# A four-layer graph network on one core: turns without loops, gather buffers of five groups, scatters in batches of five groups

## The chip, the cores and the metric

The kernel runs on one core of a Trainium2 chip. The metric is the device time of one execution in microseconds (us); less is better. The core has five engines that each work through their own queue in order: TensorE (PE, with its weight loads listed as PEld), VectorE (DVE), ScalarE (ACT), GpSimd (POOL) and SyncE (SP), which here only starts DMAs. Indirect DMAs (gathers and scatters by a list of row numbers) are issued by POOL, all others by SP.

## What is computed

A graph has N = 12500 nodes with 32 features each and E = 400000 edges (`src`, `dst`), sorted by `dst`. Four message-passing layers follow each other, each with a residual and a layer norm:

```python
edge_index = jnp.stack([src, dst])
x = _layernorm(x + _L0_gnn_ref(x, edge_index, edge_weight1, edge_attr_3, edge_attr_5, L0_gnn_W), axis=-1)
x = _layernorm(x + _L1_gnn_ref(x, edge_attr_2, L1_gnn_weight, edge_index), axis=-1)
x = _layernorm(x + _L2_gnn_ref(x, edge_index, edge_attr_2, L2_gnn_g, L2_gnn_mu, L2_gnn_sigma, L2_gnn_root, L2_gnn_bias), axis=-1)
x = _layernorm(x + _L3_gnn_ref(x, edge_weight, edge_attr_3, edge_index, L3_gnn_w1, L3_gnn_b1, L3_gnn_w2, L3_gnn_b2), axis=-1)
```

Layers 0, 2 and 3 read a row of `x` per edge at `src` and add a message at `dst`: layer 0 multiplies the row with spherical harmonics of the edge and mixes by small matrices, layer 2 weighs it by three Gaussians of the edge's two attributes (and takes a mean, a root matrix and a bias), layer 3 multiplies it with a matrix that a small network makes from the edge's distance. Layer 1 goes the other way:

```python
# _L1_gnn_ref
xj = x[edge_index[1]]                       # rows at dst
msg = basis[:, 0:1] * (xj @ w2[0])
for k in range(1, k1 * k2):                 # 16 products of tent functions
    msg = msg + basis[:, k:k + 1] * (xj @ w2[k])
out = jax.ops.segment_sum(msg, edge_index[0], num_segments=n_nodes)   # added at src
```

## The kernel before

An edge tile is P = 128 edges; T = 5 tiles are a group, G = 25 groups a turn, and NG = 25 turns are all edges. Since the edges are sorted by target, the targets of a group fit in a window of W = 64 nodes; a wider group would be done again under `If(wide)` (L469), which this data never enters.

**Layers 0, 2 and 3** share `edge_pass` (L330). `begin(i)` copies the turn's source indices, relative targets and window starts from tables of the whole graph (`src_all`, `rel_all`, `base_i`) into small tiles by DVE (L343, L345, L349; two buffers each) and calls the layer's `prepare`. For every group, `gathered` (L352) has POOL gather 5 x 128 rows of `x` into an `xg` tile (L356; six buffers). In layers 0 and 2, ACT copies `xg` to PSUM as `xp` (L414). `one_hot` has DVE make the group's 128 x 64 target one-hots (`hot`, L372; four buffers); layer 0 also stores them to HBM, `hot_d`, from where layer 3 loads them. DVE makes the per-edge product (layer 0: `prod`, L625 and L631; layer 2: L855), PE multiplies it with the one-hots (L386), and DVE adds the result to the running sums in SBUF, `acc`, at a column that it reads from the base tile (L406).

Layer 0's `prepare0` also computes the basis of layer 1, in `basis_rows` (L575): `d` on DVE (L579), two activations on ACT (L585, L586), `basis` on DVE (L589), transposes on PE (L604), copies on ACT (`bs`, L608 to L611), and stores to `basis_d` by SP. Layer 3 has a radial network on PE (`pr`, L971, biases set by ACT at L966), a product and a sum on DVE (L986, L998), and runs one group ahead.

The turns are in a hardware loop over NG // U, with U = 5 turns written out inside:

```python
def turns(j):
    begun = begin(j * U)
    for k in range(U):
        now = begun
        for s in range(G):
            if s == G // 2 and k + 1 < U:
                begun = begin(j * U + k + 1)
            yield j * U + k, s, now

with tc.For_i(0, NG // U, 1) as j:
    run(turns(j))
```

**Layer 1** first multiplies every node's row with all 16 matrices (`y_d`). Then `turn1` (L697) goes through a turn. For each group SP loads basis rows (`bas`), relative targets (`rel`), five slices of `y_d` (`yw`, at offsets read from `pairs`) and source rows (`row`). ACT copies `rel` to PSUM (`rel_p`, L723; one buffer), DVE makes basis-weighted one-hots from it (`bm`, L726, two per group), PE multiplies them with `yw` (`pe`, L744, ten matmuls), ACT copies the messages (`msg`, L752). Edges of one tile with an equal source are summed by PE (`pm`, L774, with `same` of L758), and all but one of such edges are sent to a spare row: DVE works out the destinations `to` (L762 to L770). ACT copies the sums (`add`, L776; four buffers), and POOL adds the five tiles to five copies of the result in HBM, `sums[t]`, by five indirect DMAs (L778). Its loop is like the one above (L786). A later pass, `node_pass`, adds the copies up.

A scheduler sets the order of the instructions on each engine when the program is built, by estimated times; waits between engines follow from which tile is read and written. Inside a loop's body it may move instructions of one turn into another, but not past the loop's ends.

Of the kernel before, what the change touches and what calls it, by code (L numbers as in the profile page):

```python
# [10 lines left out]
F32 = mybir.dt.float32  # L11
I32 = mybir.dt.int32
AF = mybir.ActivationFunctionType
ALU = mybir.AluOpType
# [6 lines left out]
P = 128  # L21
F = 32
T = 5
G = 25
W = 64
U = 5
V = 16
EPS_LN = 1e-5

# [10 lines left out]
def kernel(  # L40
# [25 lines left out]
    nc = tc.nc  # L66
    N = x_in.shape[0]
    NG = src_t.shape[0]
    GT = G * T
# [27 lines left out]
        out=before,  # L97
        in_=before,
        compare_op=ALU.is_gt,
        fill=0.0,  # L100
        base=0,
# [8 lines left out]
    base_i = const.tile([1, NS], I32, name="base_i")  # L110
    src_all = const.tile([P, NG, GT], I32, name="src_all")
    rel_all = const.tile([P, NG, GT], F32, name="rel_all")
# [52 lines left out]
    nid = const.tile([P, 2], F32, name="nid")  # L165
# [89 lines left out]
    with (  # L255
# [10 lines left out]
        for c, n in ((0, 124), (1, 124)):  # L266
# [10 lines left out]
            for idx, (_, _, lo) in enumerate(COMBOS):  # L277
                for k in range(3 if lo else 1):
                    to = wc0[:n, c, 8 + k : F : 3] if lo else wc0[:n, c, 0:8]
# [39 lines left out]
    src_c = nodes.tile([P, GT], I32, name="src_c")  # L319
    rel_c = nodes.tile([P, G, T], F32, name="rel_c")  # L320
    base_c = nodes.tile([1, G], I32, name="base_c")
# [8 lines left out]
    def edge_pass(layer, pools, acc, prepare, product, chunks, xg_psum=False):  # L330
# [5 lines left out]
        io, work, ps_agg, ps_x = pools  # L336
# [2 lines left out]
        nc.vector.memset(acc, 0.0)  # L339

        def begin(i):
            src = io.tile([P, GT], I32, name="src")
            nc.vector.tensor_copy(src, src_all[:, ds(i, 1), :].rearrange("p a g -> p (a g)"))  # L343
            rel = io.tile([P, G, T], F32, name="rel")
            nc.vector.tensor_copy(  # L345
                rel.rearrange("p g t -> p (g t)"), rel_all[:, ds(i, 1), :].rearrange("p a g -> p (a g)")
            )
            base = io.tile([1, G], I32, name="base")
            nc.vector.tensor_copy(base, base_i[:, ds(i * G, G)])  # L349
            return src, rel, base, prepare(i)  # L350

        def gathered(s, begun):  # L352
            xg = work.tile([P, T, F], F32, name="xg", bufs=6)
            src = begun[0]
            for t in range(T):
                nc.gpsimd.indirect_dma_start(  # L356
                    out=xg[:, t, :],
                    out_offset=None,
                    in_=x_dram[layer],
                    in_offset=bass.IndirectOffsetOnAxis(  # L360
                        ap=src[:, s * T + t : s * T + t + 1], axis=0
                    ),
                )
            return xg

        def one_hot(i, s, begun, first):
            hot = work.tile([P, T, W], F32, name="hot", bufs=4)
            kept = hot_d[ds(i * G + s, 1)].rearrange("a p t w -> (a p) t w")
            if first and layer == 3:
                nc.sync.dma_start(hot, kept)  # L370
                return hot
            nc.vector.tensor_tensor(  # L372
                hot,
                iota_w[:, None, :].to_broadcast([P, T, W]),
                begun[1][:, s, :, None].to_broadcast([P, T, W]),
                ALU.is_equal,
            )
            if first and layer == 0:
                nc.sync.dma_start(kept, hot)
            return hot  # L380
# [14 lines left out]
        def add_up(s, begun, agg, adds):  # L395

            with tc.issue_after(adds[-1].ins) if adds else nullcontext():
                at = nc.values_load(
                    begun[2][0:1, s : s + 1],
                    engines=[DVE],  # L400
                    min_val=0,
                    max_val=N,
                    skip_runtime_bounds_check_because="a target's index or N, by the min below",
                )
            cols = acc[:, :, ds(at, W)]
            adds.append(nc.vector.tensor_tensor(cols, cols, agg, ALU.add))  # L406

        def run(groups, first=True):
            adds = []
            for i, s, begun in groups:  # L410
                xg = gathered(s, begun)
                if xg_psum:
                    xp = ps_x.tile([P, T, F], F32, name="xp")
                    nc.scalar.copy(xp, xg)  # L414
                    xg = xp
                hot = one_hot(i, s, begun, first)
                prod = product(begun[3], i, s, xg)
                add_up(s, begun, aggregate(prod, hot), adds)
# [28 lines left out]
        if isinstance(product, tuple):  # L447
            run = run_ahead

        def turns(j):  # L450
            begun = begin(j * U)
            for k in range(U):
                now = begun
                for s in range(G):
                    if s == G // 2 and k + 1 < U:
                        begun = begin(j * U + k + 1)
                    yield j * U + k, s, now

        with tc.For_i(0, NG // U, 1) as j:
            run(turns(j))  # L460


        wide = nc.values_load(
# [4 lines left out]
        )  # L468
        with tc.If(wide > 0):  # L469
            with tc.For_i(0, NG, 1) as i:  # L470
                src, rel, base, _ = begin(i)
                nc.vector.tensor_copy(rel_c, rel)
                nc.vector.tensor_copy(src_c, src)
                nc.vector.tensor_copy(base_c, base)
                n_win = nc.values_load(
                    wins_i[0:1, ds(i, 1)],
                    min_val=1,
                    max_val=(N - 1) // W + 1,
                    skip_runtime_bounds_check_because="a span of targets, which are below N",
                )  # L480
                with tc.For_i(0, n_win, 1):
                    nc.vector.tensor_scalar(rel_c, rel_c, float(W), None, op0=ALU.subtract)
                    nc.vector.tensor_scalar(
                        base_c, base_c, float(W), float(N), op0=ALU.add, op1=ALU.min
                    )
                    prep = prepare(i)
                    run([(i, s, (src_c, rel_c, base_c, prep)) for s in range(G)], first=False)
# [79 lines left out]
    with ExitStack() as sums_es:  # L567
      acc0 = sums_of(sums_es, 0, 124, 2)
      with ExitStack() as es:
        pools = layer_pools(es, 0)  # L570
        io, work = pools[:2]
# [50 lines left out]
        def product0(sh, i, s, xg):  # L622
# [14 lines left out]
            return prod  # L637

        edge_pass(0, pools, acc0, prepare0, product0, [(0, 124), (124, 248)], xg_psum=True)
      node_pass(0, acc0, [wc0[:124, 0, :], wc0[:124, 1, :]])  # L640

# [6 lines left out]
    sums = [dram.tile([N + P, F], F32, name=f"sums{t}") for t in range(T)]  # L648
    with ExitStack() as es:
        io = es.enter_context(tc.tile_pool(name="yio", bufs=2))  # L650
# [34 lines left out]
    with ExitStack() as es:  # L685
        io = es.enter_context(tc.tile_pool(name="io1", bufs=2))
        one = es.enter_context(tc.tile_pool(name="one1", bufs=1))
        work = es.enter_context(tc.tile_pool(name="work1", bufs=2))
# [5 lines left out]
        def load_pairs(i, to):  # L694
            nc.sync.dma_start(to, pair_d[ds(i * GT, GT)].rearrange("(a t) -> a t", a=1))

        def turn1(i, pairs, ids):  # L697
            src_f = ps_s.tile([P, G, T], F32, name="src_f")
            nc.vector.tensor_copy(
                src_f.rearrange("p g t -> p (g t)"), src_all[:, ds(i, 1), :].rearrange("p a g -> p (a g)")  # L700
# [3 lines left out]
                spare, past[:, None, :].to_broadcast([P, G, T]), src_f, ALU.subtract  # L704
            )
            for s in range(G):
                e0 = i * (G * SE) + s * SE

                def spread(of):
# [10 lines left out]
                rel = work.tile([P, T, P], F32, name="rel", bufs=3)  # L720
# [45 lines left out]
                nc.vector.tensor_reduce(later, dup, AX.X, ALU.max)  # L766
                to_f = work.tile([P, T], F32, name="to_f")
                nc.vector.tensor_tensor(to_f, later, spare[:, s, :], ALU.mult)
                to = work.tile([P, T], I32, name="to", bufs=4)
                nc.vector.tensor_tensor(to, to_f, src_f[:, s, :], ALU.add)  # L770

                pm = ps_m.tile([P, T, F], F32, name="pm")
                for t in range(T):
                    nc.tensor.matmul(pm[:, t, :], same[:, t, :], msg[:, t, :], start=True, stop=True)  # L774
                add = work.tile([P, T, F], F32, name="add", bufs=4)
                nc.scalar.copy(add, pm)  # L776
                for t in range(T):
                    nc.gpsimd.indirect_dma_start(  # L778
                        out=sums[t],
                        out_offset=bass.IndirectOffsetOnAxis(ap=to[:, t : t + 1], axis=0),  # L780
                        in_=add[:, t, :],
                        in_offset=None,
                        compute_op=ALU.add,
                    )

        with tc.For_i(0, NG // U, 1) as j:  # L786
            for k in range(U):
                i = j * U + k
                pairs = io.tile([1, GT], I32, name="pairs")
                load_pairs(i, pairs)  # L790
                turn1(i, pairs, nid)


        over = nc.values_load(
# [26 lines left out]
    with ExitStack() as sums_es:  # L821
      acc2 = sums_of(sums_es, 2, 97, 1)
      with ExitStack() as es:
        pools = layer_pools(es, 2)
        io, work = pools[:2]
        one = es.enter_context(tc.tile_pool(name="one2", bufs=1))
# [42 lines left out]
    with ExitStack() as sums_es:  # L869
      acc3 = sums_of(sums_es, 3, 80, 1)  # L870
      with ExitStack() as es:
        pools = layer_pools(es, 3, agg_bufs=1, x_bufs=0)
        io, work = pools[:2]
# [253 lines left out]
```

## Time and profile before

| | us |
|---|---|
| median of 3 runs | 19965.96 |
| lowest and highest | 19964.43, 19989.18 |
| profiled execution | 19970.15 |
| its span, first to last instruction | 19968.4 |

Busy time in the profiled span:

| engine | busy us | share | instructions |
|---|---|---|---|
| PE | 12304.1 | 62% | 51816 |
| DVE | 9989.9 | 50% | 17389 |
| ACT | 3741.9 | 19% | 8543 |
| POOL | 13975.9 | 70% | 12511 |

The span falls into stages, which can be told apart by the lines that run: layer 0 from 117.69 to 4299.60 us, layer 1 from 4678.56 to 10782.50 (with the layer norm and the making of `y_d` before it), layer 2 from 10892.36 to 14860.70, layer 3 from 15055.40 to 19882.70. Shares of the whole span hide which engine is full in which stage, so the profile is read by stage. In a timeline, each line has the start, the duration, the engine, the line of the program, what it writes and reads, and in brackets how long the engine had been idle and what ended that; `issue` means that the profile shows no event that it waited for.

### The profile page before, as it was taken

Reading aid. Unit: us, or ns where it says so; the run is one execution under the profiler, and the core shown is the slowest. Engines: PE = TensorE matmul, PEld = TensorE weight load, DVE = VectorE, ACT = ScalarE, POOL = GpSimd, SP = SyncE. Lnnn points to the kernel's source line nnn. Section 1 sums busy time; section 2 is a strip of 40 time slices with the busy share of each in tenths; the row PEclk is TensorE's granted clock in tenths of the full one; section 3 lists DMA queues with packets and bytes.
Section 4 is the critical chain, followed back from the end, with each engine's and each line's share of the span. In section 5 each row is a group of like instructions: output and inputs, shape, how many; then the busy total and the mean of one; then the engine's idle time right before and its main releaser. Section 6 shows DMA issues by size and latency. Waiting matters only on the chain. (4 is left out here: it accounts for less than half of the span.)

```text
span 19968.4 us, 200494 instructions
## 1 busy us (share of the span) xinstructions
PE 12304.1 (62%) x51816; PEld 9777.9 (49%) x51817; DVE 9989.9 (50%) x17389; ACT 3741.9 (19%) x8543; POOL 13975.9 (70%) x12511
## 2 busy tenths in 40 slices
PE   4666667677767767677674222222246767777776
PEld 4666666665666666666664222222233333333333
DVE  3333333323444444444444222222229999999998
ACT  0000000001111111111110000000004545445454
POOL 5777767745878878788786777777756665666664
PEclk9975555555555555555555555555556777777777
DMA  2121211115766767677674000000002222222222
GB/s 57 46 50 45 49 47 48 48 55 134 129 123 129 129 122 129 123 129 129 122 129 91 14 15 14 15 15 14 14 11 56 56 58 53 60 55 58 55 58 48
DMA packets 1944708, 1361.88 MB, mean 68 GB/s; under 512 B 1123399, under 2 KB 1691663, under 8 KB 1938192
## 3 DMA queue, kind: packets, MB, share of 16 engines
q1 hardware_dynamic: 1193443, 1142.31, 21.9%
q0 software_dynamic: 750000, 205.60, 11.9%
q8 instruction: 441, 7.23, 0.2%
q14 instruction: 824, 6.75, 0.1%
HBM read 1127.27 MB, written 219.34 MB: 67 GB/s over the span
## 5 line engine op out<-in xcount | busy, mean ns | idle before, releaser
L356 POOL DMA_INDIRECT xg<-x,src x6250 | 6112.7, 978 | 2938.6 <-issue 1480.4
L386 PE MATMUL agg<-hot,prod 128*124 128x64 f32 (+1 forms) x18750 | 3868.7, 400 | 4161.7 <-DVE prod L855 2822.5
L778 POOL DMA_INDIRECT sums<-add,to x3125 | 4863.3, 1556 | 1645.1 <-issue 1084.5
L386 PEld LDWEIGHTS agg<-hot,prod 128*124 128x124 f32 (+1 forms) x18750 | 3686.5, 309 | 4351.0 <-issue 4285.4
L356 POOL DMA_INDIRECT xg<-in_x_in,src x3125 | 2998.6, 960 | 1232.2 <-issue 792.3
L744 PE MATMUL pe<-yw,bm 128*128 128x32 f32 x12500 | 2926.3, 403 | 1460.1 <-DVE bm L726 1403.1
L744 PEld LDWEIGHTS pe<-yw,bm 128*128 128x128 f32 x12500 | 2758.2, 328 | 1629.7 <-DVE bm L726 1495.6
L971 PE MATMUL pr<-wr,h 64*128 64x512 f32 x6250 | 2800.5, 926 | 821.0 <-ACT pr L966 735.2
L726 DVE SCALAR_TENSOR_TENSOR bm<-rel_p,nid,bas 128x640 f32<-128x640 f32 x1250 | 1090.6, 881 | 3253.4 <-ACT rel_p L723 3253.4
L406 DVE TENSOR_TENSOR acc<-acc,agg 124x128 f32 (+2 forms) x1875 | 448.7, 239 | 3215.8 <-PE agg L386 3211.0
L971 PEld LDWEIGHTS pr<-wr,h 64*128 64x128 f32 x6250 | 968.5, 275 | 2090.4 <-ACT pr L966 1353.4
L986 DVE TENSOR_TENSOR big<-pr,fa 128x1024 f32<-128x1024 f32 x1875 | 1838.3, 1032 | 24.1 <-ACT fa L958 20.0
L966 ACT COPY pr<-b2r 128x1024 f32<-128x1024 f32 x1875 | 1594.1, 872 | 1076.4 <-DVE big L986 1035.1
L998 DVE TENSOR_REDUCE msg<-big 128x160 f32<-128x2560 f32 x625 | 1754.2, 2807 | 0.2
L414 ACT COPY xp<-xg 128x160 f32<-128x160 f32 x1250 | 370.3, 296 | 7242.7 <-DMA xg<-x,src 3654.2
L774 PE MATMUL pm<-msg,same 128*128 128x32 f32 x6250 | 1464.7, 403 | 272.0 <-ACT msg L752 272.0
L774 PEld LDWEIGHTS pm<-msg,same 128*128 128x128 f32 x6250 | 1380.5, 329 | 356.2 <-ACT msg L752 356.2
L855 DVE TENSOR_TENSOR prod<-gauss,xp 128x480 f32<-128x480 f32 x625 | 408.5, 654 | 1890.9 <-ACT xp L414 1842.4
L386 PEld LDWEIGHTS agg<-hot,msg 128*80 128x80 f32 x6250 | 596.8, 177 | 1220.6 <-DVE acc L406 1187.0
L386 PE MATMUL agg<-hot,msg 128*80 128x64 f32 x6250 | 692.3, 268 | 570.0 <-DVE acc L406 538.5
L752 ACT COPY msg<-pe 128x160 f32<-128x160 f32 x625 | 182.8, 293 | 3734.3 <-PE pe L744 3734.3
L372 DVE TENSOR_TENSOR hot<-consts,rel 128x320 f32<-128x320 f32 x1250 | 601.4, 484 | 176.6 <-DMA hot_d<-hot 176.6
(166 smaller groups left out, 7408.1 us busy)
## 6 DMA issues: line engine op xcount, KB each, us to landing
bas<-basis_d SPq DMA_DIRECT2D x625, 320.0 KB
rel<-rel_d SPq DMA_DIRECT2D x625, 320.0 KB
row<-in_src_n SPq DMA_DIRECT2D x625, 320.0 KB
hot_d<-hot SPq DMA_DIRECT2D x625, 160.0 KB
yw<-y_d SPq DMA_DIRECT2D x3125, 32.0 KB
xg<-x,src POOLq DMA_INDIRECT x6250
hot<-hot_d SPq DMA_DIRECT2D x625, 160.0 KB
dist<-in_ew_n SPq DMA_DIRECT2D x625, 96.0 KB
```

The lines of the kernel that those rows point to most:

```text
L356: nc.gpsimd.indirect_dma_start(out=xg[:, t, :], out_offset=None, in_=x_dram[layer], in_offset=bass.IndirectOffsetOnAxis(ap=src[:, s * T + ...
L372: nc.vector.tensor_tensor(hot, iota_w[:, None, :].to_broadcast([P, T, W]), begun[1][:, s, :, None].to_broadcast([P, T, W]), ALU.is_equal,)
L386: nc.tensor.matmul(agg[:, c, :], prod[:, t, a:b], hot[:, t, :], start=(t == 0), stop=(t == T - 1),)
L406: adds.append(nc.vector.tensor_tensor(cols, cols, agg, ALU.add))
L726: nc.vector.scalar_tensor_tensor(bm[:, h], rel_p, ids[:, h : h + 1], bas, op0=ALU.is_equal, op1=ALU.mult)
L744: nc.tensor.matmul(pe[:, t, :], bm[:, h, t, :], yw[:, t, h * F : (h + 1) * F], start=(h == 0), stop=(h == 1),)
L774: nc.tensor.matmul(pm[:, t, :], same[:, t, :], msg[:, t, :], start=True, stop=True)
L778: nc.gpsimd.indirect_dma_start(out=sums[t], out_offset=bass.IndirectOffsetOnAxis(ap=to[:, t : t + 1], axis=0), in_=add[:, t, :], in_offset ...
L966: nc.scalar.copy(pr[:, : b - a, :], b2r.rearrange("p o u j -> p (o u j)")[:, None, :].to_broadcast([P, b - a, 512]),)
L971: nc.tensor.matmul(pr[:, k, :], h[64 * k : 64 * k + 64, a // 2, :], wr[64 * k : 64 * k + 64].rearrange("h o u j -> h (o u j)"), start=Fals ...
L986: nc.vector.tensor_tensor(big[:, a * 4 : b * 4], pr[:, : b - a, :].rearrange("p t (o u j) -> p (t o) u j", u=8, j=16), fa[:, a * 4 : b * 4 ...
L998: nc.vector.tensor_reduce(msg[:, :, 0:32], big.rearrange("p (t o) u j -> p t (o u) j", o=4), AX.X, ALU.add,)
```

## The change

All 25 turns are written out in all four layers, and no loop is left on the path that the data takes. `begin` makes no copies: gathers, one-hots and window starts are read from the whole-graph tables. The `xg` buffers hold five groups each and there are three of them, so 15 groups in place of six. Layer 0 has eight `hot` buffers. In layer 1 the scatters of five groups are issued together, 25 in a row, each made to depend on the last `add` and the last `to` of the five; `adds` and `tos` hold five groups in three buffers each. Only the first five groups of all are still added one by one.

```diff
-U = 5
+B = 5
...
         def begin(i):
-            src = io.tile([P, GT], I32, name="src")
-            nc.vector.tensor_copy(src, src_all[:, ds(i, 1), :].rearrange("p a g -> p (a g)"))
-            rel = io.tile([P, G, T], F32, name="rel")
-            nc.vector.tensor_copy(
-                rel.rearrange("p g t -> p (g t)"), rel_all[:, ds(i, 1), :].rearrange("p a g -> p (a g)")
-            )
-            base = io.tile([1, G], I32, name="base")
-            nc.vector.tensor_copy(base, base_i[:, ds(i * G, G)])
-            return src, rel, base, prepare(i)
+            rel = rel_all[:, i, :].rearrange("p (g t) -> p g t", t=T)
+            return src_all[:, i, :], rel, base_i[:, i * G : (i + 1) * G], prepare(i)
+
+        batch = [None]

         def gathered(s, begun):
-            xg = work.tile([P, T, F], F32, name="xg", bufs=6)
+            if s % B == 0:
+                batch[0] = work.tile([P, B, T, F], F32, name="xg", bufs=3)
+            xg = batch[0][:, s % B]
...
-            hot = work.tile([P, T, W], F32, name="hot", bufs=4)
+            hot = work.tile([P, T, W], F32, name="hot", bufs=8 if layer == 0 else 4)
...
-        with tc.For_i(0, NG // U, 1) as j:
-            run(turns(j))
+        run(turns())
...
+        def after(ins, other):
+            tc.add_manual_dep(
+                ins.ins,
+                other.ins.name,
+                mybir.DependencyInfo(mybir.DependencyClass.Sync, mybir.DependencyReason.DATA),
+                reason="one wait for what several would be waited for",
+            )
...
+                if s % B == 0:
+                    adds = work.tile([P, B, T, F], F32, name="adds", bufs=3)
+                    tos = work.tile([P, B, T], I32, name="tos", bufs=3)
+                    ready = []
+                add, to = adds[:, s % B], tos[:, s % B]
...
-                to = work.tile([P, T], I32, name="to", bufs=4)
-                nc.vector.tensor_tensor(to, to_f, src_f[:, s, :], ALU.add)
+                to_i = nc.vector.tensor_tensor(to, to_f, src_f[:, s, :], ALU.add)
...
-                add = work.tile([P, T, F], F32, name="add", bufs=4)
-                nc.scalar.copy(add, pm)
-                for t in range(T):
-                    nc.gpsimd.indirect_dma_start(
...
+                ready.append((nc.scalar.copy(add, pm), to_i))
+                if len(ready) < (1 if first and s < B else B):
+                    continue
+                for k in range(s % B + 1 - len(ready), s % B + 1):
+                    for t in range(T):
+                        into = nc.gpsimd.indirect_dma_start(
+                            out=sums[t],
+                            out_offset=bass.IndirectOffsetOnAxis(ap=tos[:, k, t : t + 1], axis=0),
+                            in_=adds[:, k, t, :],
+                            in_offset=None,
+                            compute_op=ALU.add,
+                        )
+                        for last in ready[-1]:
+                            after(into, last)
+                ready = []
...
-        with tc.For_i(0, NG // U, 1) as j:
-            for k in range(U):
-                i = j * U + k
-                pairs = io.tile([1, GT], I32, name="pairs")
-                load_pairs(i, pairs)
-                turn1(i, pairs, nid)
+        for i in range(NG):
+            pairs = io.tile([1, GT], I32, name="pairs")
+            load_pairs(i, pairs)
+            turn1(i, pairs, nid, first=i == 0)
```

`turns` now runs over all NG turns, and the body under `If(wide)` makes its own copies of the indices.

## The prediction

> **What bounds the kernel now.** I read first the busy time by stage, cutting the span where the work changes. Columns: stretch, its length, busy time (with count) of PE, PEld, DVE, ACT and POOL, granted PE clock, DMA share, GB/s. The four long rows are layers 0, 1, 2, 3; what lies between and around them sums to 887 us.
>
> ```profile
> 117.69:4299.60 4181.91, 2792.70 (x12900) 2684.58 (x12900) 1416.26 (x2622) 296.74 (x805) 2998.57 (x3125) 0.64 0.19 47
> ...
> 4678.56:10782.50 6103.94, 4383.40 (x18718) 4131.58 (x18718) 2685.12 (x4414) 742.33 (x1871) 4863.30 (x3125) 0.50 0.70 126
> ...
> 10892.36:14860.70 3968.34, 1163.95 (x6250) 1066.84 (x6250) 891.09 (x2042) 203.60 (x655) 2973.58 (x3125) 0.50 0.09 14
> ...
> 15055.40:19882.70 4827.30, 3477.72 (x12490) 1562.94 (x12486) 4737.31 (x7986) 2414.71 (x5007) 3121.03 (x3106) 0.72 0.25 56
> ```
>
> Layers 0 and 2 look alike: POOL has 3125 gathers and nothing else is near full. Layer 3 is DVE's (4737 of 4827 us). In layer 1 no engine is full. Then I read POOL's timeline (start, duration, what, idle before it and what ended that).
>
> ```profile
> 953.92 0.97 POOL L356 DMA_INDIRECT xg<-in_x_in,src  x1 [27.81 <-DVE base L349]
> 955.20 0.94 POOL L356 DMA_INDIRECT xg<-in_x_in,src  x1 [0.30 <-issue]
> ...
> 1793.33 0.97 POOL L356 DMA_INDIRECT xg<-in_x_in,src  x1 [27.76 <-DVE base L349]
> ...
> 12480.24 0.94 POOL L356 DMA_INDIRECT xg<-x,src  x1 [10.16 <-DVE base L349]
> 13275.24 0.94 POOL L356 DMA_INDIRECT xg<-x,src  x1 [10.15 <-DVE base L349]
> ...
> 16973.85 0.94 POOL L356 DMA_INDIRECT xg<-x,src  x1 [52.46 <-DVE base L349]
> 17941.94 0.95 POOL L356 DMA_INDIRECT xg<-x,src  x1 [51.87 <-DVE base L349]
> ```
>
> A gather is 0.945 + 0.303 us = 1.25, so a loop iteration of 625 takes POOL 780 us at best. The iterations are 839.4 (layer 0), 795.0 (2) and 968.1 (3). At every loop boundary POOL stands still until DVE has copied the new turn's indices (`base` L349 is the last of those copies).
>
> **The change, part by part.**
>
> Layer 0. Above 3125 x 1.25 = 3906 us the stage has 249 us of POOL idle and slow gathers before its end tail. From the timeline: four boundaries of 27.7 to 27.8 behind a first iteration, 109.8 us with what follows each; 20 stalls of up to 6.7 us, one in nearly every turn, 96.1 us; gathers of 2 to 3 us in place of 0.945, 49.6 us. The stall is this:
>
> ```profile
> 2119.70 0.24 DVE L343 COPY src<-src_all 128x125 int32 x1 [26.14 <-DMA xg<-in_x_in,src]
> 2130.64 0.94 POOL L356 DMA_INDIRECT xg<-in_x_in,src  x1 [6.27 <-ACT xp L414]
> ```
>
> The copy of the next turn's indices may not overwrite `src` before the gathers that read it have landed. DVE is in order, so `prod` behind the copy is late, `xp` of ACT waits for `prod`, and the six `xg` tiles fill. The change removes the copies (the gathers read `src_all`) and puts 15 groups in `xg`. The consumer needs 5.56 us a group where it isn't waiting, against POOL's 6.25, so it catches up 17 us in a turn, and 15 groups cover 94 us. I take off the boundaries (no loop: -110) and the stalls (-96); the slow gathers stay. One more wait could hold one-hots: their stores queue on SP behind the 12 to 16 stores of `basis_d`, up to 25 us in the waits (DVE hot <- DMA hot_d<-hot). Eight tiles of `hot` cover 8 x 6.25 = 50 us of that.
>
> Start of layer 0. The first gather is at 117.69, because `base` is copied after all of the preamble on DVE; in the changed program's order it waits only for the load of `src_all` (in by about 25 us, an estimate from the first DVE work on a load, at 25.41). 75 gathers can run before the first buffer must be free: 25 + 94 = 119. What DVE does meanwhile may slow them, and here a rule must be weighed. By the trace, some gathers are slow beside DVE operations that read two operands in SBUF: at 968.93 one takes 2.94 us beside `basis` (2.23 us). The preamble has some 15 us of such operations, all now beside gathers: `rel_all` 3.40, `rel_p` 3.49, and `d` (1.2) three times and `basis` (2.2) twice. So the 76th gather comes at about 135. The Trainium skill (SBUF — State Buffer, "Who interferes with whom") says otherwise: a tensor_tensor with both inputs in SBUF takes only the read interface of the shared ports, and descriptor generation, which needs the write interface, is inferred to go on. By that rule it is 125, set by ACT's fifth `xp` copy, which follows the memset of `acc` (93.2 to 114.2 before). I take the row: 135; should the 21 us memset hold gathers too, which nothing here shows, 155. Before, the 76th gather was at 117.69 + 94 + 5 = 217. So -82 (-62 to -92). Layer 0: -110 - 96 - 82 = -288.
>
> Layer 1. POOL's waits in the page read `issue`, which looks like overhead that batching would save. The timeline says otherwise:
>
> ```profile
> 8012.62 0.15 DVE L770 TENSOR_TENSOR to<-to_f,src_f 128x5 int32<-128x5 f32 x1
> 8013.50 1.55 POOL L778 DMA_INDIRECT sums<-add,to  x1 [0.60 <-issue]
> ...
> 8020.67 0.70 ACT L723 COPY rel_p<-rel 128x640 f32<-128x640 f32 x1
> ...
> 8022.20 0.15 DVE L770 TENSOR_TENSOR to<-to_f,src_f 128x5 int32<-128x5 f32 x1
> ...
> 8023.09 1.55 POOL L778 DMA_INDIRECT sums<-add,to  x1 [0.59 <-issue]
> ```
>
> A group's first scatter comes 0.73 us after its `to` has ended, in nearly every group. Had POOL been the bound, that lag would grow. The pitch is 9.59 us; five scatters are 5 x (1.556 + 0.303) = 9.30. What gives 9.59 is a loop through ACT's queue: `add` of group s (0.29), `rel_p` of s+1 (0.70), wait for `bm` and `pe` (5.97), `msg` (0.29), wait for `pm` (2.43): 9.7 with the overlaps. The waits carry it:
>
> ```profile
> ACT msg L752 <- PE pe L744: 3728.4, 624, 6.1
> ```
>
> Inside a turn the changed program keeps ACT, DVE, PE and SP in this same order, so the pitch stays and one wait for 25 scatters in place of five waits is worth nothing: 25 x 1.859 + 0.29 = 46.8 us per batch against 5 x 9.59 = 47.95. It nearly reaches it: scatters of over 1.6 us busy would make POOL the bound. POOL has nothing else queued, nobody but ACT and DVE wants the tiles back, and three buffers leave them two batches of room. Two changes remain: the four boundaries (25.9 to 27.4 idle in POOL) go, -106; and the last batch starts only when its fifth group is ready, so 25 scatters (46.5) follow it instead of five (9.3), +37. Layer 1: -69. Bounds: if half of each boundary comes back because SP's loads can't run ahead, -16; if the last groups' scatters cost nothing extra, -106.
>
> Layer 2: four boundaries of 8.6 to 10.2, -38. The 24 us of slow gathers stay.
>
> Layer 3: an iteration is 968.1 where five undisturbed turns of 190.2 make 951; the POOL gap of 52 us is covered by gathers that ran ahead, and DVE loses about 18 in refilling. Four times, -72; the three copies per turn (0.23, 0.22, 0.17, overlapping to 0.4) are on DVE, the bound, 25 times: -10. Layer 3: -82.
>
> Between the stages the loads of layer 1's first turn and the preparations of layers 2 and 3 no longer stand behind a loop's entry: -5, -8 and -8, guesses from how long the first group of each took. The tail of 85.7 stays.
>
> Sum: -288 - 5 - 69 - 8 - 38 - 8 - 82 = -498. From the profiled execution's 19970: 19472; the median is 4 below the profiled time, so **19468**.
>
> **The rivals.**
> A, layer 1 really is POOL's, and the 0.29 us in front of each group's first scatter is a cost of the wait. Then batching saves 4 of 5 in 625 groups: 500 x 0.29 = -145, giving 19323. For it: 9.30 is within 3% of 9.59. Against: the constant lag. 0.08.
> B, layer 0 gets a new wait for the one removed: scheduled early, `basis` stores hold one-hot stores or ACT's `xp` copies by more than the buffers cover, so that the stalls (96) stay and the early start (82) is given back: 19646. For it: ACT and SP stay in order, and the turn's basis work is compact. Against: the catch-up of 17 us a turn. 0.14.
> C, slower: instruction supply. The straight program is five times as long. Its place would be POOL in layers 0 and 2 and DVE in layer 3; it decides once such stalls there exceed 498 us. The page's instruction queues moved 7.23 + 6.75 MB in 1265 packets, so 0.4 us a packet would do it, if all fell on the path: 20,000 and above. Against: [...]POOL's pitch stays 1.25 through it. The Trainium skill (Runtime: NRT & Kernel Launch, "Instruction fetch mechanics") says that prefetch is sequential and a taken branch breaks it, which favours straight code; 0.04.
> D, it doesn't do what it says: layer 1's batching moves nothing but the end. That is inside my main case.
>
> **How the numbers follow.** Main case 0.74, its own range 19390 to 19545 (start of layer 0 -20 to +20, its stalls half kept +48, boundaries half kept in layer 1 +53, layer transitions 21). A 0.08, B 0.14, C 0.04. The range 19370 to 19620 leaves out A, most of C and the upper half of B. A measurement of this kernel can tell about 0.2% (40 us) from no change; A, B and the main case are all faster by more: 0.94 with a rest for mixtures, same 0.02, slower 0.04.
>
> **What would show it.** Right: POOL's first gather near 25 us and layer 0 ending near 4010; no gap of over 8 us on POOL in layers 0 and 2; in layer 1 a pitch of still 9.59 us a group, POOL idle about 1 us before each 25 scatters, and 46 us of scatters after the last `add`; DVE's turns of layer 3 all near 190. Wrong: a pitch near 9.3 (A), POOL waiting for `xp` in each turn of layer 0 (B), or gathers with `issue` gaps of over 0.3 (C).

## The result, and the profile after

The changed kernel takes 20174.94 us (median of four runs, 20174.11 to 20175.7) beside 19965.19 for the kernel before: 1.0103 times as long, 95% interval 1.0085 to 1.0120. It is slower by 210 us where the prediction said 498 us faster. Measured once more (e7), the ratio was 1.0101 (1.0084 to 1.0118). Of the later runs, e1 to e6, e11 to e14, e17 and e18 were disturbed: the kernel before itself took 22003 to 22397 us beside them, because DVE waited up to 31 us at a time (45 in e4) for late results of PE in stretches of layers 0, 2 and often 3, so their totals compare only beside the same before, and stages or groups outside such stretches are read instead.

Busy time by stage in the profile after; the stretches are layers 0, 1, 2 and 3, columns as in the prediction's first block:

```profile
9.82:4011.80 4001.98, 2787.67 (x12904) 2682.41 (x12904) 1489.38 (x2630) 292.18 (x801) 3001.40 (x3126) 0.64 0.21 52
4385.54:10420.20 6034.66, 4386.06 (x18718) 4134.23 (x18718) 2685.19 (x4414) 737.78 (x1871) 4854.89 (x3125) 0.50 0.72 128
10529.14:14456.00 3926.86, 1165.15 (x6250) 1067.43 (x6250) 871.27 (x1957) 198.14 (x649) 2969.89 (x3125) 0.50 0.09 14
14654.77:20088.70 5433.93, 3903.90 (x12466) 1772.59 (x12466) 4758.82 (x7905) 2386.73 (x4998) 2962.45 (x3101) 0.60 0.21 50
```

Measured the same way in both traces (layer 0 up to its last `acc` add, layer 1 and 2 from POOL's first instruction to the start of its last, layer 3 from the first `acc` add to the last; the two rows between are what lies between those marks):

| stage | before | after | difference | predicted |
|---|---|---|---|---|
| start to end of layer 0 | 4299.3 | 4011.5 | -288 | -288 |
| layer 0 to 1 | 379.3 | 374.0 | -5 | -5 |
| layer 1 | 6102 | 6033 | -69 | -69 |
| layer 2 with what leads to it | 4074 | 4032 | -42 | -46 |
| layer 2 to 3 | 211.1 | 204.7 | -6 | -8 |
| layer 3 | 4817 | 5434 | **+617** | **-82** |

Five rows are within a few us of the forecast, though that of layer 0 hits its sum by luck (see below). All of the miss is layer 3. There DVE is busy 4759 us as before (4737), but that is no longer nearly the whole stage: it idles 675 us of 5434. The timeline of a middle group of layer 3 after, with POOL, SP and weight loads left out of the copy:

```profile
17003.60 0.71 ACT L952 ACTIVATE h<-dist,hb,hw 128x384 f32<-128x384 f32 x1 [2.82 <-PE pr L984]
17004.21 0.21 ACT L969 COPY fa<-fa 128x40 f32<-128x40 f32 x1
...
17004.45 0.23 ACT L971 ACTIVATE fa<-fa 128x40 f32<-128x40 f32 x1
17004.72 2.95 DVE L999 TENSOR_TENSOR big<-pr,fa 128x1024 f32<-128x1024 f32 x3 [0.70 <-ACT fa L971]
...
17005.97 1.02 ACT L979 COPY pr<-b2r 128x1024 f32<-128x1024 f32 x1 [1.29 <-DVE big L999]
...
17007.04 5.49 PE L984 MATMUL pr<-wr,h 64*128 64x512 f32 x10 [2.04 <-ACT pr L979]
...
17012.57 0.71 ACT L952 ACTIVATE h<-dist,hb,hw 128x384 f32<-128x384 f32 x1 [3.69 <-PE pr L984]
...
17016.01 4.62 PE L984 MATMUL pr<-wr,h 64*128 64x512 f32 x10 [1.96 <-ACT pr L979]
```

Read it as a ring. `big` (DVE) of one group starts; after its first third a `pr` bank is free, ACT writes the biases into it (1.02), PE runs ten matmuls (5.49), then ACT computes `h` (0.71), then the three small `fa` copies, and the next `big` waits for the last of them. Intervals of 8.96 and 8.10 us alternate from group to group, as the ten matmuls take 5.49 and 4.62, and once a turn an interval of 13.7 holds the preparation of the next turn as well; a turn takes 218.45 us, where an undisturbed one took 190.2. The `h` in the ring is not this group's: it is that of the group three ahead. There are three `h` buffers, so it overwrites the one that the current `pr` reads, and must wait for PE. ACT is in order, so the copies of `fa` wait behind it. The waits of layer 3 say so, first before, then after (us in total, times, longest):

```profile
ACT h L939 <- DMA dist<-in_ew_n: 1016.6, 607, 4.1
...
DVE big L986 <- ACT fa L958: 20.0, 51, 1.9
```

```profile
ACT h L952 <- PE pr L984: 1988.6, 620, 3.7
...
DVE big L999 <- ACT fa L971: 669.5, 593, 1.6
```

Before, `h` waited for its data 607 times and never for PE's `pr`, and `big` lost 20 us to `fa`, not 670. The built order, in which the scheduler puts the instructions on each engine, shows the reason: `h` stands three groups ahead of the `fa` beside it in 637 of 650 groups (625, and 25 in the body under `If(wide)`). In the loop of before it stood two ahead, in 610 of the 625 groups by the trace.

### The profile page after: what moved, and what is told of

It is laid out like the page before. It is cut to its first block, busy times and chain, and to the rows that moved or that the text cites. A ratio compares the mean times of both kernels' runs of the same rounds, so it can differ in the third digit from the quotient of the medians.

```text
span 20172.2 us, 184797 instructions
## 1 busy us (share of the span) xinstructions
PE 12733.9 (63%) x51816; PEld 9989.8 (50%) x51817; DVE 10026.0 (50%) x17164; ACT 3705.2 (18%) x8536; POOL 13813.2 (68%) x12511
## 3 DMA queue, kind: packets, MB, share of 16 engines
q8 instruction: 425, 6.96, 0.2%
q14 instruction: 634, 5.19, 0.1%
## 5 line engine op out<-in xcount | busy, mean ns | idle before, releaser
L353 POOL DMA_INDIRECT xg<-x,src_all x6250 | 5955.8, 953 | 3606.3 <-issue 1945.9
L790 POOL DMA_INDIRECT sums<-adds,tos x3125 | 4854.9, 1554 | 1561.0 <-issue 1136.5
L984 PE MATMUL pr<-wr,h 64*128 64x512 f32 x6250 | 3141.8, 1037 | 1280.1 <-ACT pr L979 1280.1
L353 POOL DMA_INDIRECT xg<-in_x_in,src_all x3125 | 3001.3, 960 | 1000.9 <-issue 920.2
L984 PEld LDWEIGHTS pr<-wr,h 64*128 64x128 f32 x6250 | 1085.0, 307 | 2698.3 <-ACT pr L979 1810.1
L383 PEld LDWEIGHTS agg<-hot,msg 128*80 128x80 f32 x6250 | 692.5, 201 | 1015.5 <-DVE acc L403 1007.1
L383 PE MATMUL agg<-hot,msg 128*80 128x64 f32 x6250 | 794.5, 295 | 295.9 <-DVE acc L403 289.3
L952 ACT ACTIVATE h<-dist,hb,hw 128x384 f32<-128x384 f32 x625 | 441.4, 706 | 1997.2 <-PE pr L984 1991.0
```

The costliest lines, as they stand in the source:

```text
L353: nc.gpsimd.indirect_dma_start(out=xg[:, t, :], out_offset=None, in_=x_dram[layer], in_offset=bass.IndirectOffsetOnAxis(ap=src[:, s * T + ...
L383: nc.tensor.matmul(agg[:, c, :], prod[:, t, a:b], hot[:, t, :], start=(t == 0), stop=(t == T - 1),)
L790: into = nc.gpsimd.indirect_dma_start(out=sums[t], out_offset=bass.IndirectOffsetOnAxis(ap=tos[:, k, t : t + 1], axis=0), in_=adds[:, k, t ...
L952: nc.scalar.activation(h, dist, AF.Relu, bias=hb, scale=hw)
L984: nc.tensor.matmul(pr[:, k, :], h[64 * k : 64 * k + 64, a // 2, :], wr[64 * k : 64 * k + 64].rearrange("h o u j -> h (o u j)"), start=Fals ...
```

## Experiments on layer 3

**One part of the change alone: layer 3 written out in the kernel before (e4).**

```diff
-        with tc.For_i(0, NG // U, 1) as j:
-            run(turns(j))
+        if layer == 3:
+            run(all_turns())          # begin(0), then 25 turns in one stretch
+        else:
+            with tc.For_i(0, NG // U, 1) as j:
+                run(turns(j))
```

> The kernel before with one part of the change alone: layer 3's turns written out (copies of the indices and six xg tiles stay). Theory S: writing out alone puts h three groups ahead, layer 3 takes 5430 to 5470 instead of 4827, total 19965 + 600 to 640 = 20565 to 20605. Rival R (the buffers of five groups, or what the earlier layers leave, are needed for it): layer 3 gains its boundaries, 4745, total 19880.

Layer 3 took 5441 us, each turn 218.4 to 218.5 after the first, as in the changed kernel to a tenth of a us. Its total was 22441.04 beside 22353.69 (1.0032, 1.0021 to 1.0044), not 600 more: it is a disturbed run, and beside it the loop form of layer 3 was slowed as well (5321 in e1), while e4's layer 3 was not. The chief wait of its layer 3:

```profile
ACT h L951 <- PE pr L983: 1920.7, 603, 3.7
```

So neither the gather buffers nor the missing copies nor the earlier layers are needed for it: writing the turns out is enough.

**Layer 3 as before, the rest changed (e1, e13, e18).** The loop of five turns, the copies and six `xg` tiles were put back for `layer == 3`.

> The changed kernel with layer 3 alone put back as it was: loop of five turns, copies of the indices, six xg tiles. Theory S (the 607 us that layer 3 lost are in layer 3 and come from how its written-out turns stand on ACT): layer 3 takes some 4830 us again instead of 5434, total 20175 - 604 = 19570 (19540 to 19600), and the h activation waits for dist, not for pr. Rival R (something that the earlier layers leave behind, a lower PE clock above all, slows layer 3): layer 3 stays at 5434 and the total near 20175.

> The kernel of e1 (layer 3 as before: loop of five turns, copies, six xg tiles; the rest changed). Theory S: layer 3 4817 to 4840, total 19540 to 19600. Rival R: 20100 or more.

> The kernel of e1 and e13 once more (only layer 3 as before). Beside a before of 19970: Theory S layer 3 4817 to 4840, total 19540 to 19600; rival R 20100 or more. Beside a before of 22000 or more: as e13, 22970.

All three were disturbed: 23198.82, 22974.74 and 23187.24 us (ratios 1.0380, 1.0416 and 1.0374), layer 3 5321, 5183 and 5325. The totals expected were missed, and totals can't decide here. What can be read is the wait and the group: `h` waits for `dist` again, not for `pr`, and the median time from one `acc` add to the next, where no late result of PE falls, is 7.32 us in e13 and 7.46 in e18, against 8.55 in the changed kernel and 7.31 before. e13's line:

```profile
ACT h L978 <- DMA dist<-in_ew_n: 1352.6, 576, 30.0
```

**Only the place of `h` on ACT changed (e2, e5, e11, e15).** The one edit is an ordering edge; `muls` collects the last `fa` instruction of every group:

```diff
-            nc.scalar.activation(h, dist, AF.Relu, bias=hb, scale=hw)
+            with tc.issue_after(muls[-3].ins) if isinstance(i, int) and len(muls) >= 3 else nullcontext():
+                nc.scalar.activation(h, dist, AF.Relu, bias=hb, scale=hw)
...
-            nc.scalar.mul(fa[:, :, 2, 0:8], fa[:, :, 1, 8:16], -1.0)
+            muls.append(nc.scalar.mul(fa[:, :, 2, 0:8], fa[:, :, 1, 8:16], -1.0))
```

> The changed kernel with one ordering edge on ACT in layer 3: the h activation of group s+3 is issued behind the last fa of group s, not ahead of its three small copies. No instruction, buffer or turn differs. Theory S: big of group s no longer waits through pr of the same group and h, a group takes 7.3 us or a little more instead of 8.74, layer 3 4650 to 4800, total 19400 to 19540. Rival B (h has too few buffers): h still waits for pr, so layer 3 stays within 100 us of 5434. Rival R: no difference either.

> The kernel of e2 once more (h of group s+3 behind the last fa of group s), on another call, because in e2 long stalls of DVE ahead of acc, which the first traces don't have, lie over the groups. Theory S: layer 3 4650 to 4800 us, a group 7.31, total 19400 to 19540. Rival B (too few h buffers): layer 3 within 100 us of 5434.

> The kernel of e2 (one ordering edge: h of group s+3 behind the last fa of group s), on a chip on which before takes 19970 us. Theory S (order on ACT): a group 7.31 instead of 8.74 us, layer 3 4600 to 4760 instead of 5433, total 19350 to 19500. Rival B (h lacks a buffer) and rival R (something left by the earlier layers): 20100 or more.

> The kernel of e2 and e11 once more. Beside a before of 19970: Theory S layer 3 4600 to 4760 instead of 5433, total 19350 to 19500; rivals B and R 20100 or more. Beside a before of 22000 or more: as e11, 24440.

e2, e5 and e11 were disturbed and gave 24602.68, 24659.45 and 24440.39 us (1.1006, 1.1029 and 1.1085), far off the expectation in total; only the median group had it, 7.32 in the undisturbed groups of e2 and of e11. e15 ran beside a before of 19963.37 and settles it: 19452.96 us, ratio 0.9745 (0.9729 to 0.9761), with a layer 3 of 4712 us in place of 5434. Its stage row and what is left of the wait of `h`:

```profile
14657.10:19369.40 4712.30, 3380.56 (x12466) 1517.59 (x12466) 4706.45 (x7905) 2404.79 (x4998) 3056.20 (x3101) 0.75 0.24 57
```

```profile
ACT h L955 <- PE pr L987: 84.8, 170, 1.6
```

DVE is busy 4706 of 4712 us: the stage is DVE's again, as it was before, without its boundaries. The traces of e15 and of the changed kernel have the same order on DVE and on POOL in layer 3, and on ACT too when `h` is left out, so on these engines nothing but `h` moved. One edge on one engine is worth 719 us (20171.68 of e7 less 19452.96; the kernels before beside them took 19969.06 and 19963.37).

PE's clock is the other half of it. The mean granted clock of layer 3 was 0.72 before, 0.60 in the changed kernel and 0.75 in e15. Groups sorted by the clock granted while their ten `pr` matmuls ran (number of groups, then medians of the matmuls' time and of the time from `big` to `big`; the group with a turn's preparation is left out):

| clock | before | changed kernel | e15 |
|---|---|---|---|
| below 0.55 | 126: 5.48, 7.31 | 298: 5.48, **8.96** | 151: 5.48, 7.31 |
| 0.55 to 0.95 | 376: 4.54, 7.31 | 300: 4.62, **8.10** | 300: 4.54, 7.31 |
| above 0.95 | 98: 3.17, 7.31 | 2: 3.54, 6.83 | 149: 3.17, 7.31 |

In the changed kernel a group takes the time of the matmuls plus 3.48 us; before and in e15 it takes DVE's 7.31 at any clock. At the full clock the ring would last 3.17 + 3.48 = 6.65 us, an estimate from these rows, and DVE would be the bound. So the order brings PE's time into the turn, and the lower clock makes that longer than DVE's. The lower clock alone costs nothing here, as the first row shows for before and e15. The full clock came in 1 to 5 groups of about 600 with this order (the changed kernel, e4, e7) and in 98 or more without it; whether the order causes that is not shown.

**`h` later still (e6).** `muls[-2]` in place of `muls[-3]`, so that no `h` waits for the current `pr`.

> As e5, but h of group s+2 (not s+3) behind the last fa of group s, so that no h has to wait for pr of the current group at all. Theory S: the same as e5 or up to 60 us less, layer 3 4650 to 4760, total 19380 to 19500. Rival: if h is now too late for pr of the next group, a group takes longer than 7.31 and layer 3 is over 4800.

24669.93 us beside 22364.59 (1.1025, 1.1007 to 1.1044), disturbed, and not told apart from e5's 24659.45 beside the same before. Whether the 85 us that `h` still waits in e15 cost anything is answered by e16 below, which has this later place: no `h` waits for `pr` there, and layer 3 takes 4712 us as in e15. DVE is busy throughout, so that wait was free.

**The rival: a fourth buffer for `h` (e3, e12, e17).** `bufs=3` became `bufs=4`.

> The changed kernel with four buffers for h instead of three. Rival B (a buffer too few): the wait of h for pr goes, layer 3 4750, total 19480. Theory S: in the built order h of group s+4 now stands where h of s+3 stood, ahead of fa of group s, and its buffer is again the one that pr of group s reads: no difference, total 20160 to 20190.

> The kernel of e3 (h in four buffers, order as the scheduler makes it: h of s+4 stands where h of s+3 stood). Theory S: no gain, layer 3 5350 to 5460, total 20090 to 20200. Rival B: layer 3 4700, total 19440.

> The kernel of e3 and e12 once more (h in four buffers). Beside a before of 19970: Theory S layer 3 5350 to 5460, total 20090 to 20200; rival B layer 3 as in e15, total 19450. Beside a before of 22000 or more: as e12, 25000.

25155.47, 25007.09 and 25166.45 us, all disturbed (1.1253, 1.1338, 1.1260). Compared with the edge beside the same before (e12 with e11), it is 567 us slower. Its groups without a late result have a median of 8.95 us in e12 (from `acc` add to `acc` add), where e11's have 7.32. Sorted by clock as above, they take 8.96 (202 groups), 8.05 (227) and, at the full clock, 7.32 (26), below the full clock again the matmuls plus 3.48. The wait that the buffer should have removed is still there:

```profile
ACT h L952 <- PE pr L984: 1399.5, 454, 4.9
```

In the built order, `h` now stands four groups ahead; with two buffers it would stand two ahead, with five, five. In the written-out layer the scheduler takes every buffer as a lead, so that the last `h` that fits has to wait for the `pr` that has just been started. With three and four buffers this was measured; with two and five only the built order says so. So it is the order, and a buffer more doesn't help. What the total with four buffers is beside an undisturbed before was not measured.

## Experiments on layers 1 and 0

e7 is the changed kernel once more, as the base for e8 to e10, which have layer 3 as in the changed kernel.

> The changed kernel itself, unedited, beside the kernel before, on the chip that the runs e1 to e6 had (before takes 22354 to 22365 us there, and PE's results come up to 29 us late in some stretches of layers 0, 2 and 3). Stage by stage, if layer 3's pace is set by the order on ACT and not by PE: layer 3 5434 to 5450 (as in e4), layers 0 to 2 as in e2, total 23250 to 23350. If PE's late results hit this order too: layer 3 over 6500, total over 24400.

It was to run where e1 to e6 had been disturbed, but ran undisturbed, so the expected totals don't apply and its numbers are those of the first result: 20171.68 us beside 19969.06, layer 3 5429.

**Layer 1's ring through ACT broken (e8).** The loads of group s+1 and the copy `rel_p` are written before `msg` of group s, and an edge keeps `msg` behind it:

```diff
+                head = fetch(i, s + 1) if s + 1 < G else fetch(i + 1, 0) if more else None
...
-                nc.scalar.copy(msg, pe)
+                with tc.issue_after(head[2].ins) if head else nullcontext():
+                    nc.scalar.copy(msg, pe)
```

> The changed kernel with layer 1's rel_p of group s+1 issued on ACT ahead of msg of group s (its loads and the copy are fetched one group ahead), nothing else. The prediction's theory for layer 1 (a loop through ACT's queue sets 9.59 us a group, POOL could do 9.30): the first scatter to the last takes 625 x 9.31 + some 50 = 5850 to 5900 instead of 6033, total 140 to 180 less than e7. Rival (POOL or the DMA queues set the pace already): 6020 to 6040.

19964.01 us, 208 less than e7 (ratio to before 0.9997, 0.9987 to 1.0006). Layer 1 takes 5823 us instead of e7's 6031, a larger gain than expected: 3125 x (1.554 + 0.303) = 5803 is all that POOL needs, and no end is added, since the last `add` now comes 109 us before the last scatter (46 in the changed kernel). POOL and ACT in a middle stretch of the changed kernel, and then POOL in e8:

```profile
8020.67 0.70 ACT L734 COPY rel_p<-rel 128x640 f32<-128x640 f32 x1
...
8023.09 1.55 POOL L790 DMA_INDIRECT sums<-adds,tos  x1 [3.40 <-issue]
8024.95 1.55 POOL L790 DMA_INDIRECT sums<-adds,tos  x1 [0.30 <-issue]
```

```profile
8004.18 1.55 POOL L794 DMA_INDIRECT sums<-adds,tos  x1 [0.30 <-issue]
8006.03 1.55 POOL L794 DMA_INDIRECT sums<-adds,tos  x1 [0.30 <-issue]
8007.89 1.55 POOL L794 DMA_INDIRECT sums<-adds,tos  x1 [0.30 <-issue]
```

In the changed kernel POOL stands idle before a batch of 25 (mostly 1.8 us, 3.4 about once a turn) and works at its own pace within it, 240 us a turn. In e8 it does not stand between batches, and a turn takes 232. That `rel_p` waited for its place on ACT, and not for its load, shows in the changed kernel's line above: ACT starts it without idle time before it. That POOL's idle time was marked `issue` didn't make it POOL's own.

**Scatters after every group again (e9).** `if len(ready) < 1:`.

> The changed kernel with layer 1's scatters issued after every group again, not after five. The prediction's theory: the pitch stays 9.59, and only the end differs, 5 scatters behind the last add instead of 25, so first to last scatter 30 to 40 us less than 6033. Rival A (each wait costs POOL 0.29, which batching saves): 625 x 0.8 x 0.29 = 145 us more.

20134.95 us, 37 less than e7; layer 1 5997, 34 us less. The pitch is unchanged and the end is shorter: the last `add` is followed by five scatters:

```profile
10372.88 0.29 ACT L785 COPY adds<-pm 128x160 f32<-128x160 f32 x1 [2.43 <-PE pm L784]
...
10382.61 1.55 POOL L790 DMA_INDIRECT sums<-adds,tos  x1 [0.30 <-issue]
```

Batching costs the 37 us of the prediction and earns nothing here; rival A, under which this run would have been 145 us slower, is refuted. Whether it would earn something once the ring is broken wasn't tried.

**The small buffers in layers 0, 2 and 3 (e10).** `xg` in six tiles of one group and `hot` in four.

> The changed kernel with the buffers of before in layers 0, 2 and 3: six xg tiles of one group and four hot tiles. Are the buffers or the missing copies and loops what layer 0 gained by? If the copies' wait was all of the stall (DVE src L343): layer 0 has the same stretches, but 30 gathers in place of 75 run ahead at the start, so it ends 45 x 1.25 = 56 us later at most. If the buffers count: POOL's waits for xp grow by 100 us or more over e7.

20195.76 us, 24 more than e7 (ratio to before 1.0114, 1.0093 to 1.0134). Layer 0 ends 21 us later than in e7, all of it at the start; after that POOL has no wait for `xp` left, with room for six groups as for fifteen. So the stalls went with the index copies, not with the buffers.

**Both orders mended (e14, e16).** The changed kernel with e6's edge, e8's order and, in the last turn, the last five groups one by one.

> The changed kernel with layer 3's h (of s+2) behind the last fa of s, layer 1's rel_p ahead of msg, and the last five groups of layer 1 scattered one by one. If both causes stand and add up: layer 3 4600 to 4760 as in e11, layer 1 5800 to 5830 as in e8, total 19140 to 19290, that is 3.4 to 4.1% less than before. If layer 1's gain was partly the place of something that layer 3 loses, less than 600 us under e7 in all.

> The kernel of e14 once more. Beside a before of 19970: layer 3 4600 to 4760, layer 1 5790 to 5830, total 19140 to 19290. Beside a before of 22000 or more: as e14, 24230.

e14 was disturbed and gave 24227.31 us (1.0985, 1.0959 to 1.1012). e16 gave 19247.22 us beside 19963.37, ratio 0.9643 (0.9627 to 0.9659): layer 1 5823, layer 3 4712. Layers 1 and 3 of e16:

```profile
4390.85:10215.40 5824.55, 4118.81 (x18708) 4038.02 (x18707) 2682.11 (x4413) 728.72 (x1870) 4854.97 (x3125) 0.50 0.74 132
14448.95:19161.31 4712.36, 3362.54 (x12468) 1516.95 (x12466) 4706.48 (x7905) 2385.21 (x4998) 3055.00 (x3101) 0.75 0.24 57
```

The two gains add up, and this version beats both kernels by over 700 us.

## Why the prediction was wrong

The step that failed is "Layer 3: -82". It took the turn of 190.2 us that DVE needs in the loop as given, and took off the boundaries and the copies. That DVE sets the pace was true of the loop's order, in which ACT has `fa` ready when DVE wants it; in the new order `fa` stands behind an `h` that waits for PE, whose matmuls are then part of the turn at the clock that they get, and a turn takes 218.45 us. For layer 1 the prediction asked whether ACT, DVE, PE and SP keep their order within a turn; for layer 3 its sum rests on DVE alone. But an engine with time to spare can become the wait when its own instructions stand in another order, and once the turns are written out the scheduler places every instruction anew, also those that the diff doesn't name. No rival covered that: C, the only one on the slow side, was instruction supply. It is refuted: the instruction queues moved less than before, 6.96 and 5.19 MB against 7.23 and 6.75 (66 bytes per instruction executed against 70, worked out from the pages), POOL's gap between gathers stayed at 0.30, and e15, just as straight, is faster.

Point by point:

- Layer 0, -288: right in sum by luck, with terms off against each other. The start gave 60, not 82. The first gather came at 9.82, not 25, but the 76th at 154.77, not 135:

```profile
9.82 1.09 POOL L353 DMA_INDIRECT xg<-in_x_in,src_all  x1 [7.96 <-DMA src_all<-in_src_t]
...
120.31 21.00 DVE L339 MEMSET acc<- 124x25128 f32 x1 [5.30 <-DMA b2s<-in_l_b]
...
154.77 0.94 POOL L353 DMA_INDIRECT xg<-in_x_in,src_all  x1 [41.36 <-ACT xp L411]
```

  The consumer was late: the memset of `acc` started at 120.31, where it had been 93.18, waiting by the profile for the load of `b2s`, which stands on SP behind the first turn's stores of `basis_d`, and those now start within the preamble. Boundaries and stalls gave 210 instead of 206 (from the 76th gather to the last), and 18 came from a shorter end that wasn't forecast. The 249 us that the prediction counts as idle and slow rest on a rounded pitch of 1.25; with 1.248 they are 256, the sum of its three parts.
- Rule against row at the start: the row held. 50 of layer 0's gathers take over 1 us, some 53 us more in all. The 75 gathers of the start took 103.6 us (9.82 to 113.41), where their pitch makes 93.6: 10 us more, not 15, and the late consumer hid them.
- Layer 1, -69: right, with its parts: the boundaries go, the pitch of 9.59 stays (239.9 us for 25 groups), and the end costs 37. e8 and e9 show both.
- Layer 2, -38: right, 41 from its first gather to its last.
- B said that the early start and the stalls would be lost again, 178 us. Its mechanism, basis stores in SP's queue, did delay the start by 20 us; the stalls did not come back.

With layer 3's order mended, e15 comes near what the prediction described: 19452.96 against 19468. Part of that is luck again: layer 3 gains 104 us there, not 82 (a turn takes 189.2, not 190.2, and no boundary is left), against the shortfall at the start.

## What to carry to other kernels

When a change rewrites a loop, compare the built order on every engine in every stage, the engines with time to spare too: on an in-order engine, one instruction that runs ahead to its last free buffer puts the wait for that buffer in front of all that follows. Here a fourth buffer let it run further ahead, and an ordering edge cured it. And before a constant wait is called overhead, look whether its distance to the instruction that feeds it stays constant: then suspect a ring of engines that wait for each other, and try to cut it at the engine that closes it.

## What was not expected of the hardware

Some gathers that POOL issues beside a DVE operation with two SBUF operands end only after that operation. In both kernels each of the 25 `basis` operations of layer 0 (2.2 us) has one such gather, which ends 0.81 to 0.84 us after it; other gathers last 0.94 in all. The longest began at 38.68 us beside `rel_all`:

```profile
38.68 4.49 POOL L353 DMA_INDIRECT xg<-in_x_in,src_all  x1 [0.30 <-issue]
...
38.96 3.40 DVE L142 TENSOR_TENSOR rel_all<-dst_all,base_bc 128x3125 f32<-128x3125 int32 x1
```

At the 2.8 us TENSOR_REDUCE of layer 3 (`msg`), which reads one operand, no gather was held in this way. The Trainium skill (SBUF — State Buffer, "Who interferes with whom") infers that a tensor_tensor with both inputs in SBUF leaves descriptor generation alone; here such gathers were held. The same section says that a DVE instruction with two SBUF inputs contends with a GpSimd instruction that reads SBUF. The gathers read their row numbers from SBUF, so that sentence fits these traces, but no run here isolates that read.

What delayed PE's results in the disturbed runs was not found.
